# Graph attention and hypergraph layers in pairs of graphs: the output's root, scaling and store between two groups of loads

## The chip, the cores and the metric

The kernel runs on one core of a Trainium2 chip. The core has five engines that run side by side and wait for each other through semaphores: TensorE (PE in the profile; PEld are its weight loads), VectorE (DVE), ScalarE (ACT), GpSimd (POOL) and SyncE (SP), which here only issues transfers. The metric is the device time of one execution in microseconds (us), lower is better, as the median of several runs.

## The reference

There are 128 graphs of 128 nodes with 512 features each, and a 0/1 adjacency for each graph. Layer 0 is an attention layer with 8 heads of 64 units, layer 1 two hypergraph convolutions (512 to 1024 to 512 features) with a layer norm between them. Each layer adds its input and ends with a layer norm:

```python
feats = einsum(X, W)                              # 8 heads of 64
dense = leaky_relu(e_self[..., :, None] + e_neigh[..., None, :], 0.2)
att = softmax(dense + NEG_BIG * (1 - A))
x = layernorm(x + relu(att @ feats + b))          # layer 0
h = layer_norm(relu(hyper(x, adj, W1, b1)), gamma, beta)
x = layernorm(x + hyper(h, adj, W2, b2) + x_in)   # layer 1
# hyper(x) = Dn * H @ (Be * H^T @ (x @ W^T)) + b, H = (adj != 0)
```

## The kernel before, in words

The graphs are worked on in 64 pairs. A pair passes through five stages of one period each, and in every period the kernel works on several pairs at once, each in a different stage. All operations are Python functions with a time in a list (`todo`): pair number plus stage (`lag`), times a nominal period of T = 38.6, plus the time within the period. The list is sorted by time and the functions are called in that order; each engine and each transfer queue then gets its instructions in exactly that order. The times decide nothing but order. A dictionary (`first`) gives other times to some steps of the first pairs. Engines take their instructions in order, and so does SP: a transfer whose data isn't ready holds up every transfer behind it.

In the order of a pair's life, with the names that the profile shows:

- Stage 0: the adjacency is loaded (a L106, its first row w L112, in blocks ab L137), x in blocks (xb L129). DVE counts the nodes' weights (w, dn, dr; dd_d is their round trip through memory, dnb what comes back) and transposes xb and ab. POOL makes the mask (neg, L377).
- Stage 1: PE computes the features in seven products (pfX, pfY, pfW; a scheme with sums xS of blocks that saves one product in eight, used for ph and py as well with sums zS and hS). ACT copies pfX out, DVE adds the parts into ft (L508). From ft DVE extracts the score columns (rows, L541); they go to memory (rd, L551) and come back spread over all partitions (nb, L569). POOL adds the mask (nb<-nb,neg L588), ACT applies the leaky step (L604), DVE takes the maxima (nm, L610).
- Stage 2: ACT takes the exponentials (L618); they are written to memory (ed, L622, one write for each graph), read back in blocks (eb, L630) and transposed by DVE (eT, L639). PE multiplies eT with ft (pav, L702). DVE divides, adds the residual and takes mean and variance (y, statsa, mva, vea), POOL takes the root (rsa, L766), ACT normalizes (y, L793).
- Stage 3: PE propagates (pz), ACT copies it out (zT, L828), the hidden product (ph) follows, h, its squares (sq: ACT L891, then POOL sums of 512, 256 and 128 columns in L903) and the output product (py). The squares' sums go to memory and back (sum_blocks L949 to L954, write_sums L959, read_sums L965).
- Stage 4: DVE scales y (L1006), PE makes pq with R, DVE adds it to o (o_sum, L1023) and takes the statistics (statso, mvo, L758 and L759). Then comes the end that is changed here: `rstds` adds epsilon on DVE (veo, L764) and takes the root on POOL (rso, L766); `o_norm` scales o on DVE (L769, one instruction for each graph of the pair); `store` writes 512 KB to the output (out, L1041) from SP's queue. The last pair has steps of its own.

Around the change, SP's order in a period before is: second ed, second eb, dd_d, xb (four transfers), ab (four), rd, nb (two), dnb, sd, x, sums_out (four), out, a, w (two), first ed, first eb. DVE's is: statistics of o, first two eT (one graph), veo, two ft sums, second two eT, two L769, last ft sum, rows. POOL's is: three squares' sums of the first graph, rso, four hS sums, three squares' sums of the second graph, mask, rsa, four masked.

Of the kernel before, what the change touches and what calls it, by code (L numbers as in the profile page):

```python
# [20 lines left out]
def kernel(  # L21
# [45 lines left out]
    nc = tc.nc  # L67
# [244 lines left out]
    LAST = PAIRS - 1  # L312
    steps = []

    def step(lag, time, since=0, until=PAIRS):

        def keep(fn):
            steps.append((lag, time, fn.__name__, range(since, until), fn, ()))
            return fn
        return keep  # L320

    def at(lag, time, fn, *args, since=0, until=PAIRS):
        steps.append((lag, time, fn.__name__, range(since, until), fn, args))
# [444 lines left out]
    def normalize(s, key, t, g):  # L768
        nc.vector.tensor_scalar(  # L769
            t, t, s["mv", key][:, g, 0:1], s["rs", key][:, g:g + 1], op0=ALU.subtract,  # L770
            op1=ALU.mult,
        )
# [146 lines left out]
    def weigh(s, i, to, start):  # L919
# [3 lines left out]
          QU, 1, until=LAST)  # L923
# [105 lines left out]
    at(4, 13.3, o_sum, 1, until=LAST)  # L1029
    at(4, 14.7, o_stats, 0, until=LAST)  # L1030
    at(4, 15.5, o_stats, 1, until=LAST)
    at(4, 17.3, rstds, "o", until=LAST)

    @step(4, 23.0, until=LAST)
    def o_norm(p, s):
        for g in range(2):
            normalize(s, "o", s["o"][:, g, :], g)

    @step(4, 31.6, until=LAST)
    def store(p, s):  # L1040
        nc.sync.dma_start(out[2 * p:2 * p + 2].rearrange("g n f -> n g f"), s["o"])  # L1041

# [79 lines left out]
    for t, fn, *args in (  # L1122
# [30 lines left out]
        (117.8, prepare_output_blocks, (slice(2, 3),)),  # L1153
        (118.1, prepare_output_blocks, (slice(3, 4),)),
        (126.5, prepare_output_block_sums, (nc.gpsimd, slice(0, 2))),
        (121.3, prepare_output_block_sums, (nc.vector, slice(2, 3))),
        (141.0, prepare_output_block_sums, (nc.vector, slice(3, 4))),
        (100.0, prepare_mean_columns, ()),
    ]
# [14 lines left out]
        ("residual", 0, 0): 97.81, ("residual", 0, 1): 97.83, ("rstds", 0, "a"): 97.84,  # L1174
        ("leaky", 1, 0, 0): 113.0, ("leaky", 1, 0, 1): 117.9, ("leaky", 1, 1, 0): 119.9,
        ("largest", 1, 0, 0): 113.1, ("largest", 1, 0, 1): 118.2, ("largest", 1, 1, 0): 120.2,
        ("masked", 1, 0, 0): 98.0, ("masked", 1, 0, 1): 98.1, ("masked", 1, 1, 0): 98.2, ("masked", 1, 1, 1): 121.5,
        ("exponential", 1, 0, 0): 119.85, ("exponential", 1, 1, 1): 126.6,
        ("squares", 0, 0, 0): 141.3, ("squares", 0, 0, 1): 141.4, ("squares", 0, 0, 2): 141.5,
        ("nodes", 2): 149.8, ("write_nodes", 2): 149.9, ("spread_nodes", 2): 150.3,  # L1180
        ("r_evict", 2): 160.4,
# [91 lines left out]
```

## Time and profile before

| | us |
|---|---|
| median of 3 runs | 2437.58 (2437.31 to 2442.28) |
| profiled execution, its own time | 2448.15 |
| its span, first to last instruction | 2446.4 |
| PE busy | 2374.2 (97%) |
| DVE busy | 2048.6 (84%) |
| POOL busy | 1805.2 (74%) |
| ACT busy | 1524.7 (62%) |
| DMA, share of 16 engines in SP's queue | 48.7% |

All times that follow are from the one profiled execution, and positions are microseconds from its span's start. The granted TensorE clock is 0.998 in it. A line like "DVE L769 TENSOR_SCALAR o<-o,mvo,rso" names engine, line of the kernel, operation, and what is written from what. In the timeline, the first number is the start, the second the time to the end of the last of so many (x2) merged instructions. PE's matmuls are pipelined and their ends are modelled: they can overlap the next start. The chain of work that ended last is followed back from the last instruction, at each step to what released it.

### The profile page before, as it was taken

What the parts mean: (1) busy time and instruction counts of PE and PEld (TensorE: products, weight loads), DVE (VectorE), ACT (ScalarE), POOL (GpSimd) and SP (SyncE); (2) the same over time, 40 slices, a digit from 0 to 9 for tenths busy, and PEclk for the clock granted to TensorE, in tenths of its full rate; (3) what the DMA queues carried; (4) which work ended last, traced back from release to release, by engine and by line L of the source; (5) the groups of instructions that cost most, each with busy time, mean ns of one, the idle gap of its engine ahead of it and who ended that gap; (6) DMA issues with size and microseconds to landing.
All of it is one profiled execution on the core that took longest, in us unless ns stands there. A gap on an engine that the chain in (4) does not pass through costs nothing.

```text
span 2446.4 us, 81036 instructions
## 1 busy us (share of the span) xinstructions
PE 2374.2 (97%) x32309; PEld 1903.2 (78%) x32309; DVE 2048.6 (84%) x4456; ACT 1524.7 (62%) x4481; POOL 1805.2 (74%) x2060
## 2 busy tenths in 40 slices
PE   7899999999999999999999999999999999999998
PEld 5787787878777777777778788787787787787886
DVE  7888788888888898887888988888888888888875
ACT  4565655656657657567566666566575575665663
POOL 5777777777777777777778777777677777777774
PEclk9999999999999999999999999999999999999999
DMA  6445554555455455445554554554545455455531
GB/s 194 121 147 146 145 131 135 147 145 147 140 146 152 139 143 148 139 139 152 137 146 140 153 147 146 147 147 138 145 148 141 140 147 140 145 146 146 146 124 49
DMA packets 432872, 347.10 MB, mean 142 GB/s; under 512 B 153176, under 2 KB 382064, under 8 KB 432496
## 3 DMA queue, kind: packets, MB, share of 16 engines
q1 hardware_dynamic: 429024, 337.46, 48.7%
q8 instruction: 255, 4.18, 0.7%
q10 hardware_dynamic: 3472, 4.47, 0.5%
q14 instruction: 121, 0.99, 0.1%
HBM read 239.08 MB, written 102.73 MB: 140 GB/s over the span
## 4 chain that ended last, share of the span: by engine, by line
DMA 31%; PE 27%; DVE 14%; POOL 13%; SPq 6%; ACT 5%; issue 4%; DVEq 0%; POOLq 0%; ACTq 0%
DMA ed<-nb 13%; DMA nb<-rd 7%; PE phX L97 6%; DMA eb<-ed 5%; DVE o L769 4%; SPq L630 4%; PE pyX L97 4%; POOL nb L588 3%; PE phW L97 3%; DMA rd<-rows 3%; DVE eT L639 3%; POOL zS L839 3%; PE pfX L97 3%; PE pyW L97 2%; POOL xS L468 2%
## 5 line engine op out<-in xcount | busy, mean ns | idle before, releaser
L903 POOL TENSOR_TENSOR sq<-sq 128x512 f32<-128x512 f32 (+2 forms) x384 | 323.0, 841 | 216.0 <-ACT sq L891 196.0
L343 ACT COPY py<-pyX 128x257 f32<-128x257 f32 x189 | 70.8, 374 | 531.7 <-PE pyX L97 481.4
L97 PEld LDWEIGHTS phX<-zS,w_sb 128*64 128x64 f32 x6144 | 345.4, 137 | 36.5 <-POOL ft L741 19.6
L97 PE MATMUL phX<-zS,w_sb 128*64 128x128 f32 x6144 | 368.2, 273 | 1.1 <-ACT ph L343 1.1
L588 POOL TENSOR_TENSOR nb<-nb,neg 128x512 f32<-128x512 f32 x256 | 319.3, 1280 | 58.5 <-DMA nb<-rd 39.8
L604 ACT ACTIVATE nb<-nb,ft 128x128 f32<-128x128 f32 x1020 | 325.6, 392 | 34.9 <-POOL nb L588 32.8
L618 ACT ACTIVATE nb<-nb,nm 128x128 f32<-128x128 f32 x1024 | 319.8, 392 | 5.0 <-DVE nm L610 4.9
L97 PE MATMUL pyW<-w_sb,hS 128*64 128x256 f32 x2016 | 241.7, 380 | 11.9 <-DVE y L934 11.8
L880 ACT ACTIVATE h<-h,vecs 128x128 f32<-128x128 f32 x768 | 241.8, 392 | 3.0 <-DVE h L865 1.5
L97 PE MATMUL pyX<-w_sb,hS 128*64 128x257 f32 x2016 | 241.5, 379 | 1.4 <-POOL hS L468 1.4
L97 PE MATMUL pyX<-w_sb,h 128*64 128x257 f32 x2016 | 240.8, 379 | 0.5 <-ACT py L343 0.5
L97 PEld LDWEIGHTS pyW<-w_sb,hS 128*64 128x64 f32 x2016 | 153.3, 136 | 83.0 <-issue 19.9
L766 POOL TENSOR_TENSOR rsa<-vea,mhalf 128x2 f32<-128x2 f32 x64 | 44.8, 701 | 226.5 <-DVE vea L764 198.7
L639 DVE STREAM_TRANSPOSE eT<-eb 128x512 f32<-128x512 f32 x252 | 164.3, 690 | 55.5 <-DMA eb<-ed 55.3
L610 DVE TENSOR_REDUCE nm<-nb 128x4 f32<-128x512 f32 x256 | 175.3, 685 | 42.3 <-ACT nb L604 39.6
L97 PEld LDWEIGHTS pyX<-w_sb,h 128*64 128x64 f32 x2016 | 150.2, 136 | 69.7 <-ACT py L343 0.9
L741 POOL TENSOR_TENSOR ft<-ft,b_bc 128x512 f32<-128x512 f32 x128 | 200.0, 1583 | 5.0 <-ACT ft L532 5.0
L97 PEld LDWEIGHTS pyX<-w_sb,hS 128*64 128x64 f32 x2016 | 149.3, 137 | 57.2 <-POOL hS L468 1.6
L1006 DVE SCALAR_TENSOR_TENSOR y<-y,rsh,bw_bc 128x512 f32<-128x512 f32 x126 | 151.1, 1237 | 15.8 <-POOL rsh L1002 15.8
L891 ACT ACTIVATE sq<-h 128x512 f32<-128x512 f32 x256 | 160.6, 628 | 2.1
L804 DVE SCALAR_TENSOR_TENSOR o<-y,b_bc 128x512 f32<-128x512 f32 x128 | 161.7, 1301 | 0.0
L468 POOL TENSOR_TENSOR hS<-h 128x512 f32<-128x512 f32 x126 | 159.1, 1284 | 0.0
(178 smaller groups left out, 5536.3 us busy)
## 6 DMA issues: line engine op xcount, KB each, us to landing
nb<-rd SPq DMA_DIRECT2D x127, 512.0 KB
ed<-nb SPq DMA_DIRECT2D x126, 512.0 KB
eb<-ed SPq DMA_DIRECT2D x504, 128.0 KB
x<-in_x_dram SPq DMA_DIRECT2D x64, 512.0 KB
out_dram<-o SPq DMA_DIRECT2D x63, 512.0 KB
xb<-in_x_dram SPq DMA_DIRECT2D x248, 128.0 KB
a<-in_adj_dram SPq DMA_DIRECT2D x64, 128.0 KB
w<-in_adj_dram SPq DMA_DIRECT2D x128, 64.0 KB
```

The lines of the kernel that those rows point to most:

```text
L97: nc.tensor.matmul(to[rows], lhs[:, rows], rhs, start=start, stop=stop, skip_group_check=True)
L468: engine.tensor_tensor(t[:, i], in0, in1, op=op)
L588: nc.gpsimd.tensor_tensor(t, t, neg[:, :, None, :].to_broadcast([P, NB, HH, B]), op=ALU.add)
L604: nc.scalar.activation(t, t, AF.Prelu, bias=s["ft"][:, g, h, 0:1], alpha=SLOPE)
L610: nc.vector.tensor_reduce(s["nm"][:, g, hs], scores(p, s, g, hs).rearrange("p b h j -> p h b j"), AX.XY, ALU.max, negate=True,)
L618: nc.scalar.activation(t, t, AF.Exp, bias=s["nm"][:, g, h:h + 1])
L639: nc.vector.transpose(s["eT"][:, g, hs, :].rearrange("p h (b i) -> p h b i", b=NB), s["eb", g][:, :, hs, :].rearrange("p b h j -> p h b j"),)
L741: nc.gpsimd.tensor_tensor(t, t, b0_bc.rearrange("p (h u) -> p h u", h=H), op=ALU.add)
L804: nc.vector.scalar_tensor_tensor(s["o"][:, g, :], s["y"][:, g, :], 2.0, b2_bc, op0=ALU.mult, op1=ALU.add)
L880: nc.scalar.activation(dst[:, k, :], src[:, k, :], AF.Relu, bias=b1_sb[:, c:c + 1])
L891: nc.scalar.activation(s["sq"][:, g, q * KH // 2:(q + 1) * KH // 2, :], hid(s, g, q), AF.Square, scale=DH ** -0.5,)
L903: nc.gpsimd.tensor_tensor(t[:, :n, :], t[:, :n, :], t[:, n:2 * n, :], op=ALU.add)
```

## The change

In stage 4 the root moves from time 17.3 to 15.6, the scaling from 23.0 to 17.0 and the store from 31.6 to 19.5. In the instruction order this has four effects in each period: veo goes ahead of the first two eT; rso goes ahead of the first graph's squares' sums on POOL; the two L769 go ahead of the first two ft sums and of the second two eT; the store goes from behind sums_out to between xb and ab. The last hundred microseconds get the same moves. PE's order is unchanged.

In the first periods, for the first pairs only: ACT's first two squares of pair 0 go behind the relus and a feature copy; the mask of pair 3 goes behind pair 1's root rsa, masked steps and two small means on POOL; pair 0's sums of squares (sum_blocks) go behind two y sums on DVE, and the write of these sums behind a load of x on SP; one masked step of pair 1 goes ahead of a weight sum on POOL; and a weight sum on DVE goes behind a sum of h, R and a maximum.

```diff
-    at(4, 17.3, rstds, "o", until=LAST)
+    at(4, 15.6, rstds, "o", until=LAST)

-    @step(4, 23.0, until=LAST)
+    @step(4, 17.0, until=LAST)
     def o_norm(p, s):
         for g in range(2):
             normalize(s, "o", s["o"][:, g, :], g)

-    @step(4, 31.6, until=LAST)
+    @step(4, 19.5, until=LAST)
     def store(p, s):
         nc.sync.dma_start(out[2 * p:2 * p + 2].rearrange("g n f -> n g f"), s["o"])
...
-        (121.3, prepare_output_block_sums, (nc.vector, slice(2, 3))),
+        (123.15, prepare_output_block_sums, (nc.vector, slice(2, 3))),
...
-        ("masked", 1, 0, 0): 98.0, ("masked", 1, 0, 1): 98.1, ("masked", 1, 1, 0): 98.2, ("masked", 1, 1, 1): 121.5,
+        ("masked", 1, 0, 0): 98.0, ("masked", 1, 0, 1): 98.1, ("masked", 1, 1, 0): 98.2, ("masked", 1, 1, 1): 120.65,
         ("exponential", 1, 0, 0): 119.85, ("exponential", 1, 1, 1): 126.6,
+        ("square", 0, 0, 0): 134.5, ("square", 0, 0, 1): 134.6,
+        ("mask", 3): 152.0, ("sum_blocks", 0): 149.75, ("write_sums", 0): 149.76,
+        ("read_sums", 0): 149.77,
```

## The prediction

> **What bounds the kernel now.** I read the page's busy shares first, then the chain, then a table of windows, then each engine's timeline in single periods. The page:
>
> ```profile
> PE 2374.2 (97%) x32309; PEld 1903.2 (78%) x32309; DVE 2048.6 (84%) x4456; ACT 1524.7 (62%) x4481; POOL 1805.2 (74%) x2060
> DMA 31%; PE 27%; DVE 14%; POOL 13%; SPq 6%; ACT 5%; issue 4%; DVEq 0%; POOLq 0%; ACTq 0%
> ```
>
> PE is busy 97%, yet the chain that ends last runs more through DMA, DVE and POOL. Windows, cut where PE starts a pair's first feature product (first number: length, second: PE busy):
>
> ```profile
> 110.10:1276.30 1166.20, 1137.47 (x15629) 911.37 (x15626) 980.66 (x2139) 737.06 (x2171) 871.72 (x992) 1.00 0.51 143
> 1276.30:1567.30 291.00, 291.00 (x4038) 231.46 (x4036) 253.75 (x553) 190.63 (x562) 225.62 (x256) 1.00 0.52 148
> 1567.30:2353.10 785.80, 772.20 (x10590) 624.27 (x10588) 666.48 (x1442) 498.03 (x1470) 587.47 (x672) 1.00 0.51 143
> ```
>
> They hold 31, 8 and 21 periods: 37.62, 36.37 and 37.42 us each. In the middle one PE never idles, so 36.37 us is PE's floor. The 60 periods took 2243.0 us, 37.38 each: 60.8 us above the floor, and that is the prize. The stretch of the chain through a slow period says what holds it up:
>
> ```profile
> 1206.03 1.30 DVE eT L639 x2
> 1207.34 2.92 DVE o L769 x2
> 1210.26 0.35 DVE ft L508
> ...
> 1210.96 1.59 DMA rd<-rows
> ...
> 1212.62 6.31 DMA nb<-rd
> ...
> 1219.00 5.00 POOL nb L588 x4
> ```
>
> This is a loop: the next pair's scores (nb) become exponentials, go out as ed, come back as eb, and end in the next eT. The root's scaling L769 stands in it only because DVE is in order: feature sum and rows queue behind it. What a late nb costs, from PE's and SP's timelines (start of the period; nb's load issued after; length): 1312.70, 10.96, 36.37; 1009.93, 12.69, 37.79; 1198.13, 14.49, 39.43. In the second, PE waits 1.20 for ACT's zT, which stands behind the leaky step, which waits for POOL's masks and so for nb. Over all 60: the 11 periods below 11.3 took 36.37; 14 at 12.4 to 12.7 averaged 37.19; 13 above 13.5 averaged 38.70. The mean is 12.60: rd issued at 10.65, landed 1.94 later (1.44 in 42 periods, about 3.1 in 18). An undisturbed period on DVE:
>
> ```profile
> 1315.21 1.31 DVE L639 STREAM_TRANSPOSE eT<-eb 128x512 f32<-128x512 f32 x2
> 1316.44 0.13 DVE L764 TENSOR_SCALAR veo<-mvo 128x2 f32<-128x2 f32 x1
> ...
> 1318.12 1.30 DVE L639 STREAM_TRANSPOSE eT<-eb 128x512 f32<-128x512 f32 x2
> 1319.34 2.18 DVE L769 TENSOR_SCALAR o<-o,mvo,rso 128x512 f32<-128x512 f32 x2
> ```
>
> The first eT never waits; the second waits for eb in the slow periods.
>
> **What the skill says.** The Trainium skill, "TensorE: Matmul & The Clock Gate", section on the array as 16 sub-arrays: ACT and DVE are strict FIFOs. The chain agrees: the ready feature sum starts only at 1210.26, when L769 ends. "SBUF — State Buffer", section "SBUF: two separate sides": DVE and GpSimd share a port pair as an exclusive lock for a whole instruction. The trace agrees: L769 takes 503 ns at least, 1490 in the median; at 1319.34 its pair ends at 1321.52, 0.28 after POOL's hS of 1319.90 + 1.34. "DMA: Bandwidth & Descriptors", section "Queues, rings and completion order": each DMA engine consumes a queue's descriptors in ring order. Nearest here: the small sd write, issued during nb's large load, lands 4.2 us later (1218.31 to 1222.50), rd 1.44 on a quiet queue.
>
> **The change, part by part,** on the period at 1312.70.
>
> Root. L764 goes ahead of the first eT: 1315.21. POOL starts rso 0.21 later (as now), 1315.42 to 1316.12; it now stands ahead of the first squares, which wait for it: 1316.1 instead of 1313.40. They take 2.63 plus about 0.1 of lock: to 1318.8. The hS sums follow; the third, needed first, ends 3.9 after their start now (1317.31 to 1321.24), so at about 1322.65. PE loads it as weights at 1322.47: a new wait of 0.2 us. From both sides: 0 if the lock costs nothing and the sums run at 1.27, 0.8 if DVE's statistics end 0.6 later, as in the slow period (3.1 after 1198.13, here 2.5 after the start), which a freed loop should end. I take 0.2. Behind the squares also wait the mask and rsa; POOL idles 198.7 us before rsa now, 3.1 per period, which covers a shift of 1.4.
>
> Scaling. L769 starts after the first eT (1316.6), with rso ready. It meets short POOL work: squares of 1.27 and 0.73 us, ending 1318.15; with the 0.28 it ends at 1318.45. Two feature sums of 0.4 bring 1319.2; PE accumulates into the bank that the second reads at 1319.78, so 0.5 to spare. The second eT runs 1319.1 to 1320.4; its heads are needed at 1320.78, 0.2 to spare. The last feature sum waits for PE's product (1319.78 + 1.06), rows follows, rd is issued at 1321.65, 8.95 after the period's start (now 9.53 here, 10.65 in the mean). An eb that lands late finds L769 done: 2.2 to 3.0 us leave the loop.
>
> Store. Its 512 KB and one issue (0.44) move from behind the sums' read to between xb's loads and ab's. SP then waits at it for L769 (about 5.75 us after the start; xb's issues end at 4.2 to 8); behind it stand ab (four issues, 1.9), rd and nb. ab isn't needed for 10 us. But rd's packets follow the store's (about 1.5 us: after the store's issue at 1443.99 the two microseconds from 1445 moved 369 and 274 GB/s) and ab's. ab's issues would end at about 8.7; now they end at 1429.69 in that period and the queue is empty from 1431.0, 1.3 later. So rd, issued at 8.95, loses 0.2 to 1; I take 0.5, bounds 0 and 2.7 (sd's 4.2 against 1.44). nb is then issued at 8.95 + 1.44 + 0.5 = 10.9, where periods cost 36.37. In 18 of 60 periods rd is held up 1.65 more: 12.55, worth 0.8 above the floor, less the 0.2 that PE waits anyway: 0.6 × 18/60 = 0.2 per period. In its old place the store leaves ed's write a shorter queue: slack, priced at nothing.
>
> So a period takes 36.37 + 0.2 + 0.2 = 36.77, 0.61 less than 37.38: 60 × 0.61 = 36.6 us.
>
> First periods. PE waits 1.86 at 69.29 for ACT's pf copy, behind two squares (0.61 + 0.63): moving these gives 1.2. Sums after y saves up to 1.0 (PE wait at 87.25), the mask after the rest frees rsa (POOL waits 3.5 for the adjacency at 87.24). But PE's 1.77 at 104.24 hangs on y L1006, queued behind R's wait for dnb (1.63), which nothing here speeds: part is lost. Bounds 0 and 4.5, I take 2. At the end the scaling delays the last but one pair's second eT: 1 us lost, bounds 0 and 2.
>
> Sum: 36.6 + 2 − 1 = 37.6 us off the profiled span of 2446.4, so 2408.8. That execution took 2448.15 itself, 10.6 over the runs' median of 2437.58; the same saving gives 2400.
>
> **Rivals.** (1) The store's data cost rd 1.5 to 2 instead of 0.5. nb goes out at about 12.2, whose neighbours average 37.0 (11 periods, 11.9 to 12.4): 0.38 × 60 = 23 saved, with the first and last periods 24: 2414. For: sd's 4.2. Against: the queue is nearly idle when rd goes. (2) Slower: rd lands like sd, 4.2 after issue behind store and ab. nb goes out at 13.15, about 37.8 (second example): 0.42 × 60 = 25 lost, less 1: 2462. It decides from a landing of 3.65, where nb is at today's 12.6. Against: ab is small (128 KB). (3) No change: L769 meets two full instructions, 1.5 each. It ends at 1319.6, the second eT at 1321.6, and PE's attention heads wait 1.0 of the 1.01 to be won: 2437. For: 1490 is the median; against: the squares beside it are shorter.
>
> **How the numbers follow.** Main case 0.62, 2384 to 2411 (the new PE wait 0 to 0.4); rival 1 0.20; rival 2 0.10; rival 3 0.08. The range 2384 to 2432 covers main and rival 1, which reaches up to nb at 12.5, and leaves out 2 and 3. A change of 0.2% (4.9 us) is about what a measurement of this kernel can tell from none. Faster 0.82; rival 3 gives 0.06 same, 0.02 slower; slower with rival 2: 0.12.
>
> **What would show it.** Right: L769 (now 4% of the chain) all but gone from it; rd at about 9 after the period's start, nb at 11; periods mostly 36.4 to 36.8; small PE waits on POOL hS. Wrong: rd to nb above 3 us in most periods (rivals 1, 2), PE waiting for ft or eT (rival 3), periods above 37.4.

## The result, and the profile after

The change makes the kernel faster by less than half of what was forecast: 2423.51 us (median of five runs, 2417.17 to 2425.23) against 2437.58 (five runs of the kernel before, 2437.31 to 2444.39). The ratio is 0.9928, with a 95% interval of 0.9908 to 0.9948. Forecast were 2400.0. The profiled execution took 2417.17 us, the shortest of the five; its span is 2415.4 us and its granted clock 0.997.

The busy shares and the chain's engines on the page of the changed kernel:

```profile
PE 2374.1 (98%) x32309; PEld 1880.3 (78%) x32309; DVE 2083.3 (86%) x4456; ACT 1524.0 (63%) x4481; POOL 1830.5 (76%) x2060
PE 49%; DVE 22%; POOL 16%; DMA 5%; ACT 4%; issue 2%; SPq 1%; POOLq 0%; DVEq 0%; ACTq 0%
PE pyX L97 13%; PE phX L97 9%; POOL hS L468 8%; PE pyW L97 8%; POOL sq L903 5%; DVE o L804 4%; PE pz L97 4%; PE phY L97 4%; PE pyY L97 4%; DVE h L865 3%; DVE statso L758 2%; ACT nb L604 2%; DVE o L1023 2%; DVE hB L434 2%; DVE nm L610 1%
```

Transfers have all but left the chain (31% to 5%), and L769 is no longer among its lines. In their place stand PE's products and, new, POOL's hS with the squares before it. Windows of the changed kernel (columns as before), cut at the first full period, the 60 periods and the end; the same cuts in the kernel before follow:

```profile
65.10:111.20 46.10, 38.79 (x509) 31.15 (x506) 39.23 (x82) 25.55 (x77) 34.48 (x35) 0.96 0.42 112
111.20:2320.90 2209.70, 2200.47 (x30246) 1744.41 (x30244) 1932.02 (x4132) 1424.42 (x4201) 1709.10 (x1920) 1.00 0.51 146
2320.90:2415.40 94.50, 84.75 (x1096) 65.84 (x1092) 61.15 (x123) 40.64 (x113) 50.53 (x60) 0.98 0.23 70
```

```profile
65.50:110.10 44.60, 37.62 (x508) 30.67 (x506) 37.22 (x81) 26.08 (x80) 34.00 (x35) 1.00 0.44 124
110.10:2353.10 2243.00, 2200.68 (x30247) 1767.11 (x30244) 1900.89 (x4132) 1425.72 (x4201) 1684.81 (x1920) 1.00 0.51 144
2353.10:2446.40 93.30, 84.50 (x1096) 65.24 (x1092) 60.81 (x123) 40.68 (x114) 50.11 (x60) 0.99 0.22 71
```

From one profile to the other, the 60 periods lose 33.3 us (36.6 were forecast), the stretch up to them gains 1.1 (2 were to be lost), and the end gains 1.2 (1 was forecast). So the span loses 31.0 where 37.6 were forecast. The rest of the miss, 17 us, lies between profiled executions and medians.

A quiet period of the changed kernel, which starts at 992.90, on DVE:

```profile
995.46 0.17 DVE L764 TENSOR_SCALAR veo<-mvo 128x2 f32<-128x2 f32 x1
995.64 1.31 DVE L639 STREAM_TRANSPOSE eT<-eb 128x512 f32<-128x512 f32 x2
996.87 1.94 DVE L769 TENSOR_SCALAR o<-o,mvo,rso 128x512 f32<-128x512 f32 x2
...
999.41 1.29 DVE L639 STREAM_TRANSPOSE eT<-eb 128x512 f32<-128x512 f32 x2
1001.09 0.43 DVE L508 TENSOR_TENSOR ft<-pf,pfW 128x264 f32<-128x264 f32 x1 [0.39 <-PE pfW L97]
1001.63 0.24 DVE L541 STREAM_TRANSPOSE rows<-ft 128x32 f32<-128x32 f32 x1
```

The same period on POOL:

```profile
995.71 0.70 POOL L766 TENSOR_TENSOR rso<-veo,mhalf 128x2 f32<-128x2 f32 x1 [5.25 <-DVE veo L764]
996.38 2.75 POOL L903 TENSOR_TENSOR sq<-sq 128x512 f32<-128x512 f32 x3
999.10 2.51 POOL L468 TENSOR_TENSOR hS<-h 128x512 f32<-128x512 f32 x2
1001.68 1.29 POOL L468 TENSOR_TENSOR hS<-hS,h 128x512 f32<-128x512 f32 x1
```

And on SP's queue:

```profile
998.84 0.41 SPq L1041 DMA_DIRECT2D out_dram<-o  x1
999.29 2.42 SPq L137 DMA_DIRECT2D ab<-in_adj_dram  x4
1001.89 0.34 SPq L551 DMA_DIRECT2D rd<-rows  x1
1003.44 1.99 SPq L569 DMA_DIRECT2D nb<-rd  x2
```

L769 ends 5.91 after the period's start (forecast 5.75), rd goes out at 8.99 (8.95), nb at 10.54. The wait that was forecast on PE's weight load is there (total us, times, longest), from the waits of the changed kernel:

```profile
PEld pyX L97 <- POOL hS L468: 15.2, 58, 0.3
```

### The profile page after: what moved, and what is told of

It is laid out like the page before. It is cut to its first block, busy times and chain, and to the rows that moved or that the text cites. A ratio compares the mean times of both kernels' runs of the same rounds, so it can differ in the third digit from the quotient of the medians.

```text
span 2415.4 us, 81039 instructions
## 1 busy us (share of the span) xinstructions
PE 2374.1 (98%) x32309; PEld 1880.3 (78%) x32309; DVE 2083.3 (86%) x4456; ACT 1524.0 (63%) x4481; POOL 1830.5 (76%) x2060
## 4 chain that ended last, share of the span: by engine, by line
PE 49%; DVE 22%; POOL 16%; DMA 5%; ACT 4%; issue 2%; SPq 1%; POOLq 0%; DVEq 0%; ACTq 0%
PE pyX L97 13%; PE phX L97 9%; POOL hS L468 8%; PE pyW L97 8%; POOL sq L903 5%; DVE o L804 4%; PE pz L97 4%; PE phY L97 4%; PE pyY L97 4%; DVE h L865 3%; DVE statso L758 2%; ACT nb L604 2%; DVE o L1023 2%; DVE hB L434 2%; DVE nm L610 1%
## 5 line engine op out<-in xcount | busy, mean ns | idle before, releaser
L903 POOL TENSOR_TENSOR sq<-sq 128x512 f32<-128x512 f32 (+2 forms) x384 | 344.3, 897 | 20.1
L766 POOL TENSOR_TENSOR rso<-veo,mhalf 128x2 f32<-128x2 f32 x63 | 44.2, 702 | 337.9 <-DVE veo L764 337.9
L97 PEld LDWEIGHTS pyW<-w_sb,hS 128*64 128x64 f32 x2016 | 144.4, 136 | 73.9 <-issue 0.3
L97 PEld LDWEIGHTS pyX<-w_sb,hS 128*64 128x64 f32 x2016 | 139.5, 136 | 79.8 <-POOL hS L468 15.2
L1006 DVE SCALAR_TENSOR_TENSOR y<-y,rsh,bw_bc 128x512 f32<-128x512 f32 x126 | 150.1, 1229 | 13.7 <-POOL rsh L1002 13.7
```

The source lines that it names most:

```text
L97: nc.tensor.matmul(to[rows], lhs[:, rows], rhs, start=start, stop=stop, skip_group_check=True)
L903: nc.gpsimd.tensor_tensor(t[:, :n, :], t[:, :n, :], t[:, n:2 * n, :], op=ALU.add)
```

## The experiments

"Before" in a row is the kernel before on the same chip in the same set of runs. The quiet period is the shortest of the 60; "above it" is the sum of what the 60 periods took beyond it; "rd late" counts the periods in which nb could be issued only more than 2 us after rd. These columns come from the one profile of each kernel. The ratio is the measured one, with its interval, and not the quotient of the two medians beside it.

| kernel | median us | before | ratio (95%) | mean period | quiet | above it | rd late |
|---|---|---|---|---|---|---|---|
| before, first profile | 2437.58 | | | 37.38 | 36.37 | 60.9 | 20 |
| before, again (8) | 2440.88, one run | 2427.99 | | 37.25 | 36.37 | 52.8 | 24 |
| changed | 2423.51 | 2437.58 | 0.9928 (0.9908 to 0.9948) | 36.83 | 36.69 | 8.5 | 21 |
| changed, again (1) | 2419.83 | 2429.05 | 0.9953 (0.9939 to 0.9966) | 36.82 | 36.69 | 7.9 | 23 |
| no first-period edits (2) | 2416.43 | 2429.05 | 0.9940 (0.9926 to 0.9954) | 36.77 | 36.67 | 5.6 | 22 |
| first-period edits alone (3) | 2432.63 | 2429.05 | 1.0015 (1.0006 to 1.0024) | 37.09 | 36.37 | 43.2 | 18 |
| store left in its place (4) | 2415.42 | 2429.05 | 0.9936 (0.9922 to 0.9949) | 36.81 | 36.67 | 8.4 | 21 |
| squares' sum behind hS (5) | 2400.10 | 2427.99 | 0.9889 (0.9859 to 0.9918) | 36.52 | 36.37 | 9.2 | 21 |
| root alone (6) | 2429.43 | 2427.99 | 1.0009 (0.9995 to 1.0024) | 37.14 | 36.79 | 20.9 | 11 |
| late sums undone (7) | 2415.69 | 2427.99 | 0.9952 (0.9935 to 0.9969) | 36.81 | 36.67 | 8.5 | 23 |
| PE shifted (9) | 2411.48 | 2428.15 | 0.9933 (0.9911 to 0.9956) | 36.67 | 36.37 | 18.5 | 48 |
| PE padded (10) | 2411.58 | 2428.15 | 0.9936 (0.9914 to 0.9959) | 36.68 | 36.68 | 0.3 | 0 |
| 5 and 7 together (11) | 2400.91 | 2428.15 | 0.9885 (0.9859 to 0.9912) | 36.55 | 36.37 | 11.0 | 21 |
| before, padded (12) | 2418.65 | 2459.32 | 0.9841 (0.9802 to 0.9880) | 36.81 | 36.68 | 7.9 | 0 |

**1. The changed kernel again**, with no edit.

> The changed kernel again, unaltered. Theory A (the loop was freed as forecast; what went wrong is the starting point, because the profiled execution of the kernel before was a slow one of a widely scattered kernel): median 2417 to 2425, profiled span 2413 to 2424, quiet periods 36.70 us each, PE waiting about 0.33 per period for POOL's hS, and the kernel before at 2437 to 2444 in its ordinary runs. Theory B (each execution of the changed kernel loses something that the one profile at hand does not show, because it was the fastest of its runs): a second profile shows many more periods above 37 than the first one's 11, and a span above 2420.

The second profile gives the same picture as the first (2209.0 us for the 60 periods, 10 of them above 37), so the changed kernel has no hidden loss. What its span has more, 2.7 us, lies outside of them: 2.1 ahead and 1.3 behind, while the 60 periods are 0.6 shorter. Whether the changed kernel is steadier than the one before isn't clear: its five runs lie within 3.4 us here, but within 8.1 in the first set, where five of the kernel before lie within 7.1. The kernel before was faster here (27 runs, 2422.07 to 2436.95) than the expected 2437 to 2444. Theory A holds in all but that figure.

**2 to 4. The parts of the change.** Root, scaling and store without the first-period edits:

```diff
-        (123.15, prepare_output_block_sums, (nc.vector, slice(2, 3))),
+        (121.3, prepare_output_block_sums, (nc.vector, slice(2, 3))),
-        ("square", 0, 0, 0): 134.5, ("square", 0, 0, 1): 134.6,
-        ("mask", 3): 152.0, ("sum_blocks", 0): 149.75, ("write_sums", 0): 149.76,
-        ("read_sums", 0): 149.77,
...
```

> Root, scaling and store moved as in the change, the first periods left as in the kernel before. Theory A (the first periods' reordering gives nothing: what PE wins up to 90 us it loses again to the late squares' sums before 111): 0 to 1.5 us faster than the changed kernel, first full period 44.6 instead of 46.1, 60 middle periods unchanged at 2205 to 2215. The forecast's rival to it (the first periods save 2 us): 2 us slower than the changed kernel.

The reverse, the first-period edits alone:

```diff
-    at(4, 15.6, rstds, "o", until=LAST)
+    at(4, 17.3, rstds, "o", until=LAST)
-    @step(4, 17.0, until=LAST)
+    @step(4, 23.0, until=LAST)
     def o_norm(p, s):
-    @step(4, 19.5, until=LAST)
+    @step(4, 31.6, until=LAST)
     def store(p, s):
```

> The first periods' reordering alone, root, scaling and store left as in the kernel before. Theory A: 0 to 1.5 us slower than the kernel before (2437.6 to 2439), first full period 46.1, middle periods 37.1 to 37.5 as before, scaling L769 still in the chain. The forecast: 2 us faster than before (2435.6).

Without them the change is 3.4 us faster than with them, and alone they make the kernel before slower, by 0.06 to 0.24%. In medians both (3.4 and 3.6 us) are more than the 0 to 1.5 expected, and both are against the forecast of 2 us saved. The five runs with and without them overlap a little (2416.76 to 2420.17 against 2413.45 to 2418.31).

The third takes the kernel of experiment 2 and leaves the store at its old time:

```diff
-    @step(4, 19.5, until=LAST)
+    @step(4, 31.6, until=LAST)
     def store(p, s):
```

> Root and scaling early, the store left behind the sums' read, the first periods as in the kernel before. Theory A (the scaling's exit from DVE's queue carries the gain, the store's place is worth nothing): the same as root, scaling and store together, within 2 us, about 2422; rd issued at 8.99 after a period's start and landed 1.44 later in quiet periods. Theory C (the store in its new place, ahead of rd, costs part of the gain): 3 to 8 us faster than with the store moved. Theory D (the store in its old place collides with ed's write): 3 to 8 us slower, eb later by 0.5 to 1.5.

It took 2415.42 against 2416.43: the store's place is worth nothing that five runs of each can tell. Theories C and D fall, and the forecast's rival 1 with them. rd landed late in 21 periods here and in 22 with the store moved.

**5. The new wait on hS taken away.** The kernel of experiment 2, with one short sum on POOL put behind the four hS sums:

```diff
-            at(3, ((17.0, 17.1, 17.2), (26.0, 27.3, 28.0))[g][level], squares, g, level)
+            at(3, ((17.0, 17.1, 23.5), (26.0, 27.3, 28.0))[g][level], squares, g, level)
```

> Root, scaling and store moved, first periods as in the kernel before, and the 128-column squares' sum of the first graph (0.46 us on POOL) put behind the fourth hS sum, so that PE's weights from hS are ready about 0.46 earlier: 9.6 after a period's start instead of 10.07, where PE asks at 9.78. Theory A (the new PE wait on hS is the whole 0.33 between the quiet period and PE's floor): PE's wait on hS gone, quiet periods 36.37, 60 periods about 2188 to 2192, in all 15 to 18 us faster than with the moves alone. Rival (another wait, ACT's zT or DVE's ft, stands right behind that on hS): quiet periods stay above 36.5 and less than 10 us are won.

2400.10 us: 16.3 below experiment 2, on a chip where the kernel before is 1.1 lower in its median; by the two ratios it is some 12 us. POOL in a quiet period, which starts at 985.25:

```profile
988.05 0.70 POOL L766 TENSOR_TENSOR rso<-veo,mhalf 128x2 f32<-128x2 f32 x1 [5.27 <-DVE veo L764]
988.72 2.15 POOL L903 TENSOR_TENSOR sq<-sq 128x512 f32<-128x512 f32 x2
990.84 2.69 POOL L468 TENSOR_TENSOR hS<-h 128x512 f32<-128x512 f32 x2
993.60 1.28 POOL L468 TENSOR_TENSOR hS<-hS,h 128x512 f32<-128x512 f32 x1
```

The third hS sum ends 9.63 after the start, instead of 10.07 in the changed kernel. PE asks for it at 9.78. The quiet period falls to PE's floor of 36.37, PE's wait on hS at pyX is gone from the waits, and the chain of this kernel is PE itself:

```profile
PE 86%; DMA 4%; DVE 4%; POOL 2%; ACT 2%; issue 1%; SPq 1%; DVEq 0%; POOLq 0%; ACTq 0%
```

So the wait on hS is the whole difference between the quiet period of the changed kernel and the floor. Together with experiment 11 this is the fastest version.

**6. The root alone**, with scaling and store at their old times:

```diff
-    at(4, 17.3, rstds, "o", until=LAST)
+    at(4, 15.6, rstds, "o", until=LAST)
```

> The root alone moved ahead of the first squares' sums; scaling and store stay where they were. Theory A (the gain comes from the scaling's leaving the loop, and the root ahead of the squares only costs the wait on hS): scaling L769 back in the chain, periods between 36.7 and 38, middle 2238 to 2250, 3 to 12 us slower than the kernel before. Rival (the root's earlier place is what frees the loop): like the changed kernel, middle 2205 to 2212.

The result is the same as the kernel before. L769 is back in the chain of this kernel:

```profile
DMA ed<-nb 8%; PE pyX L97 8%; PE phX L97 6%; POOL hS L468 6%; DMA nb<-rd 5%; PE pyW L97 5%; POOL sq L903 4%; ACT nb L604 3%; DMA eb<-ed 3%; DVE o L804 3%; PE phY L97 3%; DVE o L769 3%; PE pz L97 3%; SPq L630 2%; PE pyY L97 2%
```

The rival falls: the root's place alone does not free the loop; with the scaling (experiment 4) it does. Theory A's size was off. The quiet period grew by 0.42, 25 us in 60 periods, with waits on hS at pyX (18.9 us on weight loads, 11.0 on matmuls), but what lies above it fell to 20.9 from 52.8. That a longer quiet period gives the loop that much more slack would explain it; it was only argued, not tested.

**7. The late squares' sums undone**, all else as in the changed kernel:

```diff
-        ("mask", 3): 152.0, ("sum_blocks", 0): 149.75, ("write_sums", 0): 149.76,
-        ("read_sums", 0): 149.77,
+        ("mask", 3): 152.0,
```

> The changed kernel with one of its first-period edits undone: pair 0's sums of squares, their write and their read are back at their old times, all other edits stay. Theory A (the late sums of squares give back what the other first-period edits win): PE's waits before pq 1.5 to 3 us shorter, the first full period 43 to 45 instead of 46.9, 2 to 4 us faster than the changed kernel. Rival (another edit costs the time, the weight sum on DVE beside POOL's masks): within 1 us of the changed kernel.

PE's line for pair 0's pq in three timelines: the changed kernel, the changed kernel again, and this one:

```profile
104.55 3.35 PE L97 MATMUL pq<-y,R 128*64 128x512 f32 x8 [4.12 <-DVE y L1006]
```

```profile
106.52 3.46 PE L97 MATMUL pq<-y,R 128*64 128x512 f32 x8 [4.86 <-DVE y L1006]
```

```profile
104.47 1.94 PE L97 MATMUL pq<-y,R 128*64 128x512 f32 x8 [3.07 <-DVE y L1006]
```

PE's first feature product starts at other times in these executions (65.15, 66.38 and 66.10), so pq is best counted from there. With the late sums it comes 39.40, 40.14 and (experiment 3) 40.95 later; without them 38.37 and (experiment 11) 38.26; with no first-period edit 38.37 to 38.76 in six profiles. So the late sums delay pq by 0.6 to 2.7 us, and the other edits win at most 0.5 in front of it: PE gets to its wait earlier, and waits longer for y L1006. The sums' read (L965), on which that y hangs, is issued 28.74 us after the same point in the changed kernel, 26.95 here and 27.39 in the kernel before.

The first full period took 44.3, as expected, but it is no clean measure. In 8 of the 14 profiles the granted clock falls to 0.5 for 3.4 or 6.8 us at about this place. The changed kernel shows it at pq, and the kernel before in its first profile doesn't (window, busy times, granted clock, DMA; then pq in the kernel before):

```profile
104.00:107.40 3.40, 2.85 (x8) 1.12 (x10) 3.40 (x4) 2.37 (x8) 3.04 (x2) 0.50 0.35 120
```

```profile
104.24 1.94 PE L97 MATMUL pq<-y,R 128*64 128x512 f32 x8 [1.77 <-DVE y L1006]
```

Where it falls to 0.5 for 3.4 us, the first full period took 46.1 and 46.9 with the late sums, and 45.3 to 45.6 with no first-period edit; where it doesn't, 44.3 here and 44.5 to 44.7 with no first-period edit (the shifted and padded kernels apart). It fell in the second profile of the unaltered kernel before too (experiment 8), so the edits alone don't bring it; what does stays open.

In medians this kernel is 4.1 us below the changed one, but on another chip, and the two ratios to the kernel before overlap; how much of the 3.4 us of experiment 2 the late sums alone explain stays open.

**8. The kernel before again**, with no edit.

> The kernel before again, unaltered, for a second profile. Theory A (the first profile of it was a slow one, and the scatter sits in the 60 middle periods, which wait for transfers): a span near 2427 with 40 to 45 us of the middle above PE's floor instead of 60.9, first and last stretch as in the first profile within 1.5. Rival (the scatter sits in the start and end, as in setting up): middle at 2243 again.

```profile
65.80:111.10 45.30, 39.11 (x509) 31.43 (x507) 38.04 (x82) 26.79 (x81) 33.71 (x34) 0.96 0.48 126
111.10:2345.80 2234.70, 2200.32 (x30244) 1776.35 (x30242) 1895.00 (x4132) 1424.74 (x4200) 1684.35 (x1920) 1.00 0.51 144
2345.80:2439.10 93.30, 84.54 (x1096) 65.42 (x1092) 60.79 (x123) 40.66 (x114) 50.10 (x60) 0.98 0.22 71
```

The windows of this second profile differ from the first one's by 8.3 us in the 60 periods and by 0.7 and 0 in the stretches around them. So the scatter between these two executions, 7.3 us in all, sits in the periods, as theory A has it. Its sizes were off: this execution too was a slow one (2440.88 against a median of 2427.99 in 17 runs beside it), with 52.8 above the floor and not 40 to 45. No execution near the median was profiled.

**9 and 10. What holds up rd.** In most kernels some 20 of 60 periods have rd landing late. The queue of PE's instructions shows why. In the period of experiment 5 that starts at 183.26, rd is issued at 192.29, and nb can go only at 195.72. From the transfers between 192.2 and 194 (queue and kind, packets, MB, share of 16 engines):

```profile
q1 hardware_dynamic: 761, 0.09, 32.4%
q8 instruction: 1, 0.02, 5.1%
q14 instruction: 1, 0.01, 1.5%
```

In the quiet period that starts at 985.25, rd goes at 994.24 and nb at 995.68; the same view from 994.2 to 996 has no instruction packet:

```profile
q1 hardware_dynamic: 694, 0.08, 29.1%
```

The Trainium skill, "Runtime: NRT & Kernel Launch", section "Instruction fetch mechanics", says that each engine's instructions are refilled in blocks of 16 KiB (256 instructions) through a DMA queue of its own, at a cost that is mostly hidden. The trace agrees with the block: four 16 KB packets per period, each about 1 us long on one DMA engine, for 1021 instructions of PE (1008 matmuls and weight loads, and 13 of its sequencer). On the cost it shows what the page doesn't speak of: the delay of a transfer that meets a packet. In the first profile of the kernel before, the 20 periods in which such a packet starts between 0.3 us before and 1.2 us after rd's issue have nb issued 2.11 us or more after rd (2.89 in the mean); in the other 40 it is 1.74 at most. In experiment 5 it is 21 periods from 2.50 up, and 39 up to 1.64. The smaller packets of q14 don't explain it: in each of the two profiles one stands at rd in four periods only.

To test it, PE's stream is shifted by 128 instructions, in the kernel of experiment 5:

```diff
         s["px"] = [bank(f"px_{p}_{g}") for g in range(2)]
+        for _ in range(64 if p == 0 else 0):
+            nc.tensor.transpose(s["px"][0][:B, :B], ident[:B, :B], ident[:B, :B])
```

> The kernel with the squares' sum behind hS, plus 64 tiny transposes (32 by 32, 128 instructions with their weight loads) on PE while it waits for the first x. Theory F (rd is held up in those periods in which a 16 KB packet of PE's instructions starts between 8.8 and 10.1 after the period's start; those packets come every 256 instructions and drift through the period): the held-up periods, 1 to 6, 9 and 47 to 60 so far, move to about 17 to 36; rd lands 1.44 to 1.5 after its issue in 47 to 60; the sum of held-up periods stays near 20 and the time within 3 us. Rival (the hold-ups belong to the place in the run, such as the first and last quarter's traffic): they stay at 1 to 6 and 47 to 60.

The held-up periods moved from 1 to 6, 9 and 47 to 60 to one block of 4 to 51; 52 to 60 are now quiet. The rival falls. The size was off: both edges moved by about 44 periods, so the packets drift by some 2.9 instructions per period (128/44), more slowly than I had assumed; 1021 is 3 short of four packets' 1024, which fits. A full round then takes 88 periods, of which about 48 are held up. The unshifted kernel happens to have only 21 of these among its 60. The shift made the 60 periods 9.4 us longer, where 3 at most were expected.

Then the packets are held in place, by 70 transposes at the start and two more in every period:

```diff
         s["pq", g] = bank(f"pq_{p}_{g}")
+        for _ in range(2 if g == 0 else 0):
+            nc.tensor.transpose(s["pq", g][:B, :B], ident[:B, :B], ident[:B, :B])
```

> The same kernel with 70 tiny transposes at the start and two more (four instructions) in every period ahead of PE's pq, so that a period has about 1024 PE instructions and the instruction packets stay nearly at one place of the period, away from rd. Theory F: rd lands within 1.7 in at least 50 of 60 periods, the excess of the middle over its quiet period falls from 9 to under 4 us, at a cost of 0 to 0.1 per period for the two transposes: 2392 to 2400. Rival (the excess has other causes): rd quiet or not, the excess stays at 7 to 12 and the time is 2400 to 2406.

rd lands early in all 60 periods (nb goes 1.43 to 1.59 after it), and 0.3 us is left above the quiet period. The windows of this kernel show PE without a gap:

```profile
113.70:2314.80 2201.10, 2201.09 (x30366) 1740.89 (x30364) 1936.14 (x4132) 1428.64 (x4201) 1711.13 (x1920) 1.00 0.51 147
```

So theory F is right in its mechanism, and both sums miss on the price of the remedy: the two transposes cost 0.31 us per period, 18.6 in all, which is more than the 9 that they save.

**11. The best of both**: the edits of experiments 5 and 7 in one kernel.

> Root, scaling and store moved, the squares' sum behind hS, and the first-period edits of the change without the late sums of squares. Theory A (those edits win nothing once the late sums are out): the same as without any first-period edit, 2398 to 2402. The forecast's rival (they save about 2 us): 2396 to 2398.

2400.91 against 2400.10, four runs each on two chips: without the late sums the first-period edits are worth nothing that these runs can tell.

**12. The kernel before, padded** with the same transposes as in experiment 10.

> The kernel before with the same 70 tiny transposes at the start and two more per period, so that the instruction packets stay away from rd; root, scaling and store as before. The two transposes cost 0.31 per period, so a quiet period is 36.68. Theory G (the held-up rd is what starts the slow periods of the kernel before; without it the loop through the scaling would run quietly): rd lands within 1.7 in 50 or more of 60 periods, the middle falls to 2201 to 2212 and the whole to 2412 to 2422. Rival (the loop feeds itself, or other late transfers start it): rd quiet, but periods still above 37 in 20 or more of 60, middle 2220 or more, the whole 2428 to 2440.

2418.65 against 2459.32 for the unpadded kernel on this chip. No rd lands late, 50 of 60 periods are within 0.06 of the quiet one, and the chain of this kernel has turned to PE with L769 (two lines further down through the edit) still in it:

```profile
PE 69%; DMA 11%; DVE 8%; POOL 6%; SPq 2%; issue 2%; ACT 1%; DVEq 0%; POOLq 0%; ACTq 0%
PE phX L97 13%; PE pyX L97 13%; PE pyW L97 7%; PE pfX L97 7%; PE phW L97 7%; DMA ed<-nb 4%; PE pq L97 4%; PE pz L97 3%; PE pav L704 3%; PE phY L97 3%; PE pfW L97 3%; PE pyY L97 3%; DMA eb<-ed 2%; DMA nb<-rd 2%; DVE o L771 2%
```

So theory G's figures came true: without packets at rd most of the slow periods of the kernel before are gone. How much of that is the packets' doing isn't separated: the two transposes also lengthen a quiet period by 0.31, and in experiment 6 a quiet period longer by 0.42 went with 20.9 instead of 52.8 above it. The change leaves the packets where they are (21 to 23 late rd) and gives the loop slack instead.

The packets meet more than rd. In the first profile of the kernel before, rd lands within 1.5 of its issue in the periods from 43 to 60, and 17 of these 18 still take 36.9 or more, because rd is issued late. There the packets stand at the second ed write, near the end of the period before. Over the 60 periods, 20 of these writes have a packet that starts between 0.3 us before and 2 us after their issue, and eb's read follows 4.24 to 5.56 us after the write (4.73 in the mean); in the other 40 it follows after 3.10 to 4.68 (3.54). Of the 20, 13 are in the periods from 42 to 59. In the padded kernel none of the 60 meets a packet. This was read from the traces; no run tested it.

## Why the prediction was wrong

The step that failed is the last one, from one execution to the median of others; some terms before it were mis-sized, and one had the wrong sign.

Right were the direction, the loop and its cure: L769 left the chain, the second eT no longer waits for it, and with the scaling moved alone with the root (experiment 4) the gain is all there. The step "a period takes 36.37 + 0.2 + 0.2 = 36.77" measured 36.83; so the middle was forecast at 2206.4 and took 2209.7. Of its terms:

- The new PE wait "I take 0.2" measured 0.33 (36.70 − 36.37, within the bounds of 0 to 0.8; the wait on the weight load itself is 0.26 in the mean). The third hS sum came at 10.07 instead of 9.95: the root's 0.70 and squares of 2.75 instead of 2.73 start from 2.81 instead of 2.72. Cost: 60 × 0.13 = 8 us. Experiment 5 shows that all of it is this wait.
- rd "is held up 1.65 more", in 18 of 60 periods, measured 1.4 more in 21 (2.92 against 1.52; the profile of the kernel before already had 1.4 more in 20), and all that lies above the quiet period is 8.5 us and not 12. The store and ab ahead of it, "I take 0.5", cost rd nothing: it lands in 1.44 to 1.5 in quiet periods. Rivals 1 and 2 fall with that.
- L769, which meets "short POOL work", was to end at 5.75 and ended at 5.91; rival 3 falls.
- The first periods, "I take 2" saved, cost 1.1 in the profile and 3.4 us in medians (experiments 1 and 2). The step that failed is "part is lost": all was lost at y L1006, and the late sums of squares, which I counted as a gain for PE ("Sums after y"), delayed the sums' read behind them, and so y. Part of the 1.1 is the clock's: pq's matmuls took 1.4 us longer, for the most part at half of it.

The largest error is the last step, "the same saving gives 2400". The profiled execution of the kernel before was 10.57 above its median, and I took a saving that I had worked out from that execution off the median. But 60.8 us above the floor is what that execution lost. The second profile of the kernel before, 7.3 shorter in all, lost 8.1 less above the same floor of 36.37 (experiment 8). By these two executions a median one had some 10.6 less to win; none was profiled. The miss of 23.5 us is made up of these 10.6, of 6.6 by which the profiled span was forecast too low (3.3 in the middle, 3.1 at the start, 0.2 at the end), and of 6.3 by which the changed kernel's median lies above its own profile, the shortest of five. Where the 6.3 sits isn't shown; what the second profile has more than the first lies outside of the 60 periods (experiment 1). The range, 2384 to 2432, held the result through rival 1's share, for a reason that was not rival 1's.

## What to carry to other kernels

When a kernel runs in a feedback loop above an engine's floor, forecast the time after the change from the floor up, and don't subtract a saving found in one execution from the median of others: what one execution lost is its own. When a short step is moved ahead of another engine's queue, look for what that pushes past its due time, and move out the one piece there that isn't needed yet: here 0.46 us of POOL work put behind its neighbours was worth about as much as the rest of the change (16.3 us of median against the 12.6 of experiment 2). A small transfer that lands late in some periods and not in others is worth a look at the packets of the instruction queues at that instant.

## What the runs showed of the hardware that I had not expected

- A 16 KB packet of PE's instructions, 1 us long on one DMA engine, puts off a 16 KB transfer that meets it by 1.4 us. With 1021 PE instructions per period, 3 short of four packets, the collision wanders through the periods; with 1024 it stays in its place (experiments 9 and 10).
- Two 32 × 32 transposes on PE (188 to 201 ns each in the records) lengthened a period by 0.31 us in a stretch in which PE never idles.
- The kernel before differs between chips (medians 2427.99 to 2459.32). Whether a kernel at PE's floor does isn't known: 2400.10 and 2400.91 come from two chips on which the kernel before agrees as well (2427.99 and 2428.15).
- In 8 of 14 profiles the granted clock fell to 0.5 for 3.4 or 6.8 us at about 104 us. In the changed kernel six of pq's eight matmuls took 1.06 to 1.12 us each there, and 0.59 to 0.64 in the first profile of the kernel before. A mean over the stretch hides it (0.96); what brings it on isn't known.
